# One written order from the attention's end on: routing ahead of dense products, and two batches' gathered expert chains in pieces between them

## The chip, the cores and the metric

The kernel runs on one core of a Trainium2 chip. The metric is the time of one execution on the device, in microseconds; several executions are made and the median is given. A profile is one execution taken by the hardware profiler: its span is the time from its first to its last instruction.

## The reference

Input `x` is 4 batches of 1024 tokens with 128 features, all in float32. Four residual blocks follow each other, each on the layer norm of `x`:

```python
x = x + attention_a(layernorm(x))   # causal softmax, 16 heads of 64, projected back to 128
x = x + ffn(layernorm(x))           # mixture of 32 experts, two per token
x = x + attention_b(layernorm(x))   # linear attention: 16 heads of 8, running sums over all 1024 tokens
x = x + ffn(layernorm(x))           # the same experts and router again
```

The expert block routes every token by a softmax over 32 logits and keeps the two largest weights. Written plainly it sums over all experts, with a weight that is zero for 30 of the 32:

```python
rw = softmax(x @ router_w.T)                 # tokens x 32
vals, idx = top_k(rw, 2)
w = zeros_like(rw).at[rows, idx].set(vals)
out = sum(x * w[:, e:e+1] @ W[e] for e in range(32))
```

Linear attention of a batch needs, at token t, the sums over all tokens up to t of that batch. The second expert block of a token needs only that token.

## The kernel before, in words

`x` lives in SBUF as one tile `x_sb`: 32 chunks of 128 tokens, eight to a batch. Four chunks are a quad (quads 0 to 7, two per batch). The program has four parts, one after the other.

**Softmax attention** (lines 489 to 837) is written in an order made by hand (`manual_schedule`). While it works on a batch, the expert block of the batch before runs between its pieces: `experts` (L214) is a generator, and each `next` issues a small step of it. A chain of `experts` has these steps: statistics and normalization (L226 to L248), router logits (L256), softmax and the two largest (L264 to L284), counting tokens per expert (L290 to L307), the place of each token in a list sorted by expert (L312 to L356), the scatter of each token's row, scaled by its weight, to its two places in a DRAM buffer `xs_d` (L374 and L384), then a pass in groups of four tiles of 128 rows, 47 tiles in all (L402 to L444: load rows, load expert weights, transpose, multiply, store to `ys_d`), then the gather of two rows per token back to `x_sb` (L449). Scatter and gather are indirect transfers issued by POOL, one for each of 16 (chunk, choice) pairs; they are put in a list `queue` and issued one at a time by whoever pops it. The pass may be held by one chain at a time (`passing`). All state of a chain is in a `Room`, of which there is one. When the attention ends, batch 2's chain has 15 of its 16 gathers left in `queue`; these gathers add to `x_sb` in the transfer itself.

**f**: the last two quads (6 and 7, batch 3) have no attention to hide under, and are done densely by `moe` (L860). For each quad it normalizes and transposes (`normed_T`, L130), computes the router and the two weights per token (L886 to L912), and then for each of its four chunks multiplies by all 32 experts, in eight products of 128x512 (four experts each, L922, each with a bank of PSUM, five banks in turn). Products 1, 4 and 6 are scaled by ACT into a tile `t` (L930) that POOL adds up (L944 to L946) and DVE adds to `x_sb` (`settle`, L871); the other five are accumulated in `x_sb` by DVE, four instructions each (L937). Between products a callback issues pieces: `fill` advances the first two `prepare` (L971, features of the linear attention for a quad: statistics L977, POOL's L983 to L986, ACT's L992, products L1010, exp, sigmoid and log with their table loads L1025 to L1033, POOL's L1039 and L1040, DVE's L1045) and pops `queue`.

**lin**: for each chunk u in order, POOL forms the outer products `kv` (L1085), PE adds them to running sums in PSUM (L1103 and L1111), DVE multiplies by the query, reduces (`num`, L1132) and divides, PE projects, and DVE adds to `x_sb` (L1152). `prepare` of later quads runs beside it. This part too has an order by hand.

**s**: the second expert block. `moe` takes quads 2 to 7 densely, 192 products, and one chain of `experts` takes batch 0. Each product issues one pop of `queue` and, when the queue is short, one step of the chain. Here the gathers go to tiles `y` of a pool `came`, and DVE adds them (L476, L481); batch 0's output is stored by L482, a dense quad's by L874.

In f and s `moe` is not under `manual_schedule`: there the layer that records the program decides the order of instructions on each engine, and it may also put work of s into lin where its inputs are ready. Each engine works through its own instructions strictly in that order. A pool's tile is taken again only when the last use of its earlier tenant is done; `reuse_waits="tile"` says that this wait is kept tile by tile.

Of the kernel before, what the change touches and what calls it, by code (L numbers as in the profile page):

```python
# [15 lines left out]
P = 128  # L16
# [4 lines left out]
def hybrid_kernel(  # L21
# [107 lines left out]

    def normed_T(pool, xnp, c0, n, nm, known=None):  # L130

        mv, rstd = known or statistics(c0, n, nm)
        xn = xnp.tile([P, n, D], F32, tag=f"xn{n}", bufs=8 // n, name=f"xn_{nm}")
        xnT = xnp.tile([P, n * P], F32, tag=f"xnT{n}", name=f"xnT_{nm}")
        for c in range(n):
            nc.vector.tensor_scalar(
                xn[:, c, :], x_sb[:, c0 + c, :], mv[:, c, 0:1], rstd[:, c : c + 1],
                ALU.subtract, ALU.mult,
            )
        for g in range(0, n, 4):  # L140
            pt = pool.tile([P, 512], F32, tag="ps1", name=f"pxn_{nm}_{g}")
            for c in range(4):
                nc.tensor.transpose(pt[:, c * P : (c + 1) * P], xn[:, g + c, :], ident)
            nc.scalar.copy(xnT[:, g * P : (g + 4) * P], pt)
        return xnT
# [711 lines left out]
    TB = 12  # L857
    ACT_GROUPS = (1, 4, 6)

    def moe(nm_, store, first=0, between=None, known=(), lag=0):  # L860
        with ExitStack() as ph:
            xnp = ph.enter_context(tc.tile_pool(name=f"xnp{nm_}", bufs=2, reuse_waits="tile"))
            mp = ph.enter_context(tc.tile_pool(name=f"mp{nm_}", bufs=3, reuse_waits="tile"))
            ps_1 = ph.enter_context(tc.tile_pool(name=f"mps1{nm_}", bufs=3, space=PSUM, reuse_waits="tile"))
            ps_e = ph.enter_context(tc.tile_pool(name=f"mpse{nm_}", bufs=5, space=PSUM, reuse_waits="tile"))
            due = []

            def settle(keep):
                while len(due) > keep:
                    xs, s, done = due.pop(0)  # L870
                    nc.vector.tensor_tensor(xs, xs, s[:, :D], ALU.add)  # L871
                    if store and done is not None:
                        b, r = divmod(done, NB)
                        nc.sync.dma_start(  # L874
                            out=out_v[b, :, r : r + 4, :], in_=x_sb[:, done : done + 4, :]
                        )

            for q in range(first, NT // 4):
                nm = f"{nm_}_{q}"
                c0 = q * 4  # L880
                xnT = normed_T(
                    ps_1, xnp, c0, 4, f"m{nm}", known[q - first] if known else None
                )
                pl = ps_1.tile([P, 512], F32, tag="ps1", name=f"pl_{nm}")
                for c in range(4):
                    nc.tensor.matmul(  # L886
                        pl[:, c * E : (c + 1) * E], xnT[:, c * P : (c + 1) * P], rwT,
                        start=True, stop=True,
                    )
                plv = pl[:, : 4 * E].rearrange("p (c e) -> p c e", c=4)  # L890
                mx = small.tile([P, 4], F32, tag="mx", name=f"mx_{nm}")
                nc.vector.tensor_reduce(mx, plv, AX.X, ALU.max)
                ex = mp.tile([P, 4, E], F32, tag="ex", name=f"ex_{nm}")
                nc.vector.tensor_tensor(
# [11 lines left out]
                for c in range(4):  # L906
                    nc.vector.max(m8[:, c, :], rwx[:, c, 0:E])
# [7 lines left out]
                for c in range(4):  # L915
                    xs = x_sb[:, c0 + c, :]
                    parts = []
                    for g in range(E // 4):
                        if between:
                            between(ps_1)  # L920
# [310 lines left out]
```

## Time and profile before

| what | us |
|---|---|
| median of three runs (lowest, highest) | 2033.25 (2030.45, 2037.73) |
| the profiled execution, its own time | 2037.51 |
| its span | 2035.8 |
| busy in the span: PE, DVE, ACT, POOL | 1890.7, 1482.9, 1234.6, 1139.5 |
| f: from 1482 to the first `cum` product | 1596.5 |
| lin: to the last `x_sb` add of L1152 | 1785.5 |
| s: to the end of the span | 2035.8 |

How to read it: a row of engine sums gives, for a stretch of the span, how long each engine was busy and how many instructions it had; "clock" is the share of TensorE's full clock that was granted. The chain of waits goes back from the last instruction to what released it, and lists what stood on that path. A row of waits says who waited for whom, how long in total, how often, and the longest single wait. In a timeline the bracket at the end of a row is the idle time before it and what ended it. Matrix products in float32 appear as two passes each, transposes as one.

### The profile page before, as it was taken

To read this page: it belongs to the slowest core of one execution; us is meant where nothing else is said; L and a number is where in the kernel's file an instruction comes from. 1 tells how busy PE (TensorE), PEld (TensorE's weight loads), DVE (VectorE), ACT (ScalarE), POOL (GpSimd) and SP (SyncE) were. 2 spreads that over 40 slices of the span, in tenths; PEclk is the share of its full clock that TensorE was granted. 3 is DMA by queue.
4 is the path that set the end of the run, shared out by engine and by line. 5 is a ranking of instruction groups with operands and counts; after the bars stand their busy time and mean duration, and the time that the engine had idled before them with its cause. 6 is when DMAs were issued, how large, how long until landed. Compare 5 with 4: busy or idle time off the path is not lost.

```text
span 2035.8 us, 33636 instructions
## 1 busy us (share of the span) xinstructions
PE 1890.7 (93%) x10066; PEld 1052.5 (52%) x10066; DVE 1482.9 (73%) x4467; ACT 1234.6 (61%) x3889; POOL 1139.5 (56%) x2080
## 2 busy tenths in 40 slices
PE   6999999999999999999999999999958898987898
PEld 3555555555555655555565555556633454543443
DVE  5777776776787677778767676777547678966788
ACT  4766666676677566766766676776526466334344
POOL 3444445444665476556745854675476566655644
PEclk9999999999999999999999999999979999997999
DMA  7000000000003310000131100003230000004300
GB/s 214 1 1 1 1 1 1 1 1 1 1 13 93 92 22 10 1 1 5 54 107 45 18 1 1 1 17 111 80 82 0 0 0 1 0 1 123 101 11 11
DMA packets 111875, 62.54 MB, mean 31 GB/s; under 512 B 5552, under 2 KB 110160, under 8 KB 111568
## 3 DMA queue, kind: packets, MB, share of 16 engines
q1 hardware_dynamic: 101936, 50.43, 8.7%
q0 software_dynamic: 9472, 8.40, 2.1%
q8 instruction: 82, 1.34, 0.3%
q10 hardware_dynamic: 288, 1.57, 0.2%
q14 instruction: 97, 0.79, 0.1%
HBM read 35.60 MB, written 24.77 MB: 30 GB/s over the span
## 4 chain that ended last, share of the span: by engine, by line
PE 64%; DVE 12%; ACT 10%; POOL 9%; issue 3%; DMA 1%; ACTq 0%; SPq 0%; POOLq 0%; DVEq 0%
PE s L598 19%; PE po L704 10%; PE pt L687 10%; PE pe_s L922 6%; DVE nmx L607 5%; ACT p L632 3%; PE pw L719 3%; PE pk L547 3%; POOL x_sb L449 2%; ACT pT L691 2%; PE pe L430 2%; PE pv L561 2%; PE cum L1103 1%; ACT p L637 1%; PE pe_f L922 1%
## 5 line engine op out<-in xcount | busy, mean ns | idle before, releaser
L607 DVE TENSOR_REDUCE nmx<-s 128x2 f32<-128x1024 f32 x512 | 604.5, 1219 | 218.5 <-PE s L598 217.8
L632 ACT ACTIVATE p<-s,nmx 128x512 f32<-128x512 f32 (+3 forms) x640 | 361.2, 575 | 311.8 <-DVE nmx L607 264.5
L598 PE MATMUL s<-kT,qT 64*128 64x512 f32 x2048 | 518.0, 619 | 8.0 <-ACT p L632 4.5
L674 POOL TENSOR_SCALAR p<-p,f,ri 128x512 f32<-128x512 f32 (+3 forms) x768 | 503.8, 673 | 0.9 <-issue 0.6
L687 PEld LDWEIGHTS pt<-ident,p 128*128 128x128 f32 x2304 | 249.9, 141 | 219.1 <-issue 91.1
L687 PE MATMUL pt<-ident,p 128*128 128x128 f32 x2304 | 335.9, 282 | 24.4 <-POOL rs L652 7.1
L691 ACT COPY pT<-pt 128x512 f32<-128x512 f32 (+3 forms) x768 | 324.4, 510 | 11.9 <-PE pt L687 9.6
L656 POOL TENSOR_TENSOR rs<-rs,f 128x2 f32<-128x2 f32 x256 | 52.1, 204 | 438.5 <-ACT f L623 409.1
L704 PE MATMUL po<-pT,va 128*64 128x256 f32 (+1 forms) x2560 | 291.1, 365 | 0.6 <-DVE oT L711 0.6
L598 PEld LDWEIGHTS s<-kT,qT 64*128 64x128 f32 x2048 | 173.3, 185 | 195.4 <-issue 94.2
L637 ACT ACTIVATE p<-s,nmx 128x128 f32<-128x128 f32 x512 | 180.7, 366 | 107.3 <-DVE nmx L607 104.6
L704 PEld LDWEIGHTS po<-pT,va 128*64 128x64 f32 x2560 | 167.0, 136 | 97.2 <-issue 32.6
L922 PE MATMUL pe_s<-we_sb,xnT_ms 128*128 128x512 f32 x384 | 186.4, 630 | 22.9 <-DVE x_sb L937 16.4
L937 DVE SCALAR_TENSOR_TENSOR x_sb<-pe_s,w_s,x_sb 128x128 f32<-128x128 f32 x480 | 141.4, 343 | 19.2 <-PE pe_s L922 14.6
L645 DVE SCALAR_TENSOR_TENSOR p<-p,qtri 128x128 f32<-128x128 f32 x512 | 144.9, 310 | 7.0 <-ACT p L637 3.9
L652 POOL TENSOR_TENSOR rs<-rs 128x2 f32<-128x2 f32 x192 | 43.9, 229 | 186.7 <-DVE ri L665 186.7
L632 ACT ACTIVATION_READ_ACCUMULATOR p<-s,nmx 128x1 f32 x640 | 139.0, 217 | 0.0
L930 ACT ACTIVATE t_s<-pe_s,w_s 128x128 f32<-128x128 f32 x288 | 82.2, 369 | 92.5 <-PE pe_s L922 75.5
L922 PEld LDWEIGHTS pe_s<-we_sb,xnT_ms 128*128 128x128 f32 x384 | 72.2, 199 | 116.3 <-issue 37.4
L944 POOL TENSOR_TENSOR t_s<-t_s,t_s 128x512 f32<-128x512 f32 x48 | 60.9, 1269 | 81.4 <-ACT t_s L930 81.1
L724 DVE TENSOR_TENSOR x_sb<-pw,x_sb 128x128 f32<-128x128 f32 x128 | 36.9, 289 | 79.8 <-PE pw L719 79.7
L719 PE MATMUL pw<-wo_sb,oT 128*128 128x128 f32 x512 | 84.5, 289 | 1.8 <-DVE x_sb L724 1.0
(302 smaller groups left out, 2669.5 us busy)
## 6 DMA issues: line engine op xcount, KB each, us to landing
xs<-xs_d SPq DMA_DIRECT2D x33, 256.0 KB, 3.1
ys_d<-ys SPq DMA_DIRECT2D x33, 256.0 KB, 2.4
we<-_ffn_expert_weights_dram SPq DMA_DIRECT2D x24, 256.0 KB, 3.6
xs_d<-zero SPq DMA_DIRECT2D x2, 3008.0 KB, 17.9
we<-_ffn_expert_weights_dram SPq DMA_DIRECT2D x45, 64.0 KB, 1.8
xs_s<-xs_d SPq DMA_DIRECT2D x11, 256.0 KB, 3.6
ys_d<-ys_s SPq DMA_DIRECT2D x11, 256.0 KB, 3.4
we_sb<-_ffn_expert_weights_dram SPq DMA_DIRECT2D x4, 512.0 KB, 6.0
```

The lines of the kernel that those rows point to most:

```text
L598: nc.tensor.matmul(st[:, h, :], self.qT[rows, self.ib * P : (self.ib + 1) * P], self.kT[rows, j * 512 : (j + 1) * 512], start=True, stop=True,
L607: nc.vector.tensor_reduce(self.nmx[:, i, :], self.s[i], AX.X, ALU.max, negate=True)
L632: nc.scalar.activation(self.p[h][:, at : at + m * P], self.s[i][:, h, : m * P], AF.Exp, bias=bias, accum_out=self.rs[:, i, h : h + 1],)
L637: nc.scalar.activation(self.p[h][:, at + m * P : at + (m + 1) * P], self.s[i][:, h, m * P : (m + 1) * P], AF.Exp, bias=bias,)
L645: nc.vector.scalar_tensor_tensor(d, d, 1.0, qtri, ALU.mult, ALU.mult, accum_out=self.rs[:, 2, h : h + 1])
L674: nc.gpsimd.tensor_scalar(w, w, self.f[:, i, h : h + 1], self.ri[:, h : h + 1], ALU.mult, ALU.mult,)
L687: nc.tensor.transpose(pt[:, c * P : (c + 1) * P], self.p[h][:, (g + c) * P : (g + c + 1) * P], ident,)
L691: nc.scalar.copy(self.pTs[h][:, g : g + m, self.col : self.col + P], pt[:, : m * P].rearrange("p (c i) -> p c i", c=m),)
L704: nc.tensor.matmul(po[h * DH : (h + 1) * DH, c0:256], va[:, jb, h, :], pTs[h][:, jb, c0:], start=(jb == 0), stop=(jb == n - 1),)
L719: nc.tensor.matmul(pw[:, :P], oTs[i][:, c * P : (c + 1) * P], wo_sb[:, pr, :], start=(i == 0), stop=(i == len(prs) - 1),)
L922: nc.tensor.matmul(pe, xnT[:, c * P : (c + 1) * P], we_sb[:, 4 * g : 4 * g + 4, :].rearrange("p e d -> p (e d)"), start=True, stop=True,)
L937: nc.vector.scalar_tensor_tensor(xs, pe[:, e * D : (e + 1) * D], w[:, c, 4 * g + e : 4 * g + e + 1], xs, ALU.mult, ALU.add,)
```

## The change

`moe` and `normed_T` go. Their work is split in two, and everything after the attention stands under `manual_schedule`.

- `routed` is a generator that computes the router of one quad in some 15 to 22 small steps. The router of the next quad is stepped once per dense product, so it lies beside the products of the quad before. Quad 6's is issued in one go at f's start, with one step of the first `prepare` after each of its own; quad 4's is issued two steps per chunk near the end of lin.
- `dense` writes the products: after each, the next router's step and a callback with the number of the product. POOL's sums follow as soon as the second tile is there, and `settle` keeps two chunks in hand.
- In f, each product steps one of two `prepare` in turn, and every fourth pops `queue`.
- In s, quads 4 to 7 are dense (128 products). Batches 0 and 1 are done by two chains, each with a `Room` of its own, stepped together after every second product; seven of eight products pop `queue`. What is left of chains and queue after the last product is issued then.
- The pools of f, lin and s have tile-wise waits; `t` has 9 buffers in f and 12 in s.

Repeated lines and blank steps of the two new functions are left out below.

```diff
-    def normed_T(pool, xnp, c0, n, nm, known=None):
...
-    TB = 12
     ACT_GROUPS = (1, 4, 6)
...
-    def moe(nm_, store, first=0, between=None, known=(), lag=0):
...
+    ctx.enter_context(tc.manual_schedule())
+    rp = ctx.enter_context(tc.tile_pool(name="rp", bufs=2, reuse_waits="tile"))
+    ready = {}
+
+    def routed(q, nm, pool, known=None):
+
+        c0 = q * 4
...
+            yield
+            yield
+            yield
+        else:
+            mv, rstd = known
...
+        pt = pool.tile([P, 512], F32, tag="ps1", name=f"pxn_{nm}")
+        for c in range(4):
+            nc.tensor.transpose(pt[:, c * P : (c + 1) * P], xn[:, c, :], ident)
+        nc.scalar.copy(xnT, pt)
+        yield
+        yield
+        yield
+        yield
...
+        mx = small.tile([P, 4], F32, tag="mx", name=f"mx_{nm}")
+        nc.vector.tensor_reduce(mx, plv, AX.X, ALU.max)
...
+        nc.scalar.activation(ex, ex, AF.Exp)
+        yield
+        yield
...
+        nc.vector.tensor_tensor(w[:, :, 0:E], rwx[:, :, 0:E], w[:, :, 0:E], ALU.subtract)
+        ready[q] = xnT, w
+
+    def dense(nm_, qs, store, pool, mp, ps_e, known, beside):
+
...
+        turn = 0
+        for i, q in enumerate(qs):
+            xnT, w = ready.pop(q)
+            nxt = iter(())
+            if i + 1 < len(qs):
+                nxt = routed(qs[i + 1], f"{nm_}_{qs[i + 1]}", pool, known[i + 1])
+            for c in range(4):
+                xs = x_sb[:, q * 4 + c, :]
+                parts = []
+                for g in range(E // 4):
...
+                    if g in ACT_GROUPS:
+                        t = mp.tile([P, 512], F32, tag="t", name=f"t_{nm_}_{q}_{c}_{g}")
...
+                        parts.append(t)
+                        if len(parts) > 1:
+                            nc.gpsimd.tensor_tensor(parts[0], parts[0], t, ALU.add)
+                    else:
...
+                    if g == 3:
+                        settle(2)
+                    next(nxt, None)
+                    beside(turn)
+                    turn += 1
...
+                due.append((xs, s, q * 4 if c == 3 else None))
+            for _ in nxt:
+                pass
+        settle(0)
...
-    def fill(pool):
-
-        banks[0] = pool
-        turn[0] += 1
-        if turn[0] in (4, 18):
-            preps.append(prepare(len(preps), pool))
-        if turn[0] % 2:
-            for p in preps:
-                next(p, None)
-        elif turn[0] > 8:
+    def on():
+
+        for e in list(sides):
+            if len(queue) <= 4 and next(e, "end") == "end":
+                sides.remove(e)
+
+    with ExitStack() as ph:
+        mp = ph.enter_context(tc.tile_pool(name="mpf", bufs=9, reuse_waits="tile"))
+        ps_f = ph.enter_context(tc.tile_pool(name="ps_f", bufs=3, space=PSUM, reuse_waits="tile"))
+        ps_e = ph.enter_context(tc.tile_pool(name="ps_ef", bufs=5, space=PSUM, reuse_waits="tile"))
+        banks[0] = ps_f
+        preps = [prepare(t, ps_f) for t in range(2)]
+
+        def fill(turn):
+
+            next(preps[turn % 2], None)
+            if turn % 4 == 3:
+                if queue:
+                    queue.pop(0)()
+                on()
+
+        qs = list(range(NT // 4 - 2, NT // 4))
+        for _ in routed(qs[0], f"f_{qs[0]}", ps_f, known[0]):
+            next(preps[0], None)
+        dense("f", qs, False, ps_f, mp, ps_e, known, fill)
+        for p in preps:
+            for _ in p:
+                pass
+        while sides or queue:
             if queue:
                 queue.pop(0)()
-            for e in list(sides):
-                if next(e, "end") == "end":
-                    sides.remove(e)
-
-    turn, preps = [0], []
-    moe("f", False, NT // 4 - 2, fill, known)
-    for p in preps:
-        for _ in p:
-            pass
-    assert not (sides or queue) and len(preps) == 2
+            on()
 
     with lin as ph:
-
-        ph.enter_context(tc.manual_schedule())
-        lp = ph.enter_context(tc.tile_pool(name="lp", bufs=3))
-        ps_c = ph.enter_context(tc.tile_pool(name="ps_c", bufs=1, space=PSUM))
-        ps_n = ph.enter_context(tc.tile_pool(name="ps_n", bufs=1, space=PSUM))
-        ps_1 = ph.enter_context(tc.tile_pool(name="ps_l", bufs=4, space=PSUM))
+        lp = ph.enter_context(tc.tile_pool(name="lp", bufs=3, reuse_waits="tile"))
+        ps_c = ph.enter_context(tc.tile_pool(name="ps_c", bufs=1, space=PSUM, reuse_waits="tile"))
+        ps_n = ph.enter_context(tc.tile_pool(name="ps_n", bufs=1, space=PSUM, reuse_waits="tile"))
+        ps_1 = ph.enter_context(tc.tile_pool(name="ps_l", bufs=4, space=PSUM, reuse_waits="tile"))
...
+        qs = list(range(NB // 4 * 2, NT // 4))
         kv = products(0)
-        ends = []
+        ends, first = [], iter(())
...
             ahead(3 * u + 2)
-
-    def pieces(pool):
-
-        banks[0] = pool
-        if queue:
+            if u == NT - 8:
+                first = routed(qs[0], f"s_{qs[0]}", ps_1)
+            next(first, None)
+            next(first, None)
+
+    for _ in first:
+        pass
+    for b, r in enumerate((room, Room(xp, "b"))):
+        sides.append(experts(b, f"s{b}", banks, queue, r, came))
+
+    def pieces(turn):
+
+        if turn % 8 != 7 and queue:
             queue.pop(0)()
-        for e in list(sides):
-            if len(queue) <= 4 and next(e, "end") == "end":
-                sides.remove(e)
-
-    for b, r in enumerate((room,)):
-        sides.append(experts(b, f"s{b}", banks, queue, r, came))
-    moe("s", True, NB // 4, pieces, lag=3)
-    assert not (sides or queue)
+        if turn % 2 and sides:
+            on()
+
+    with ExitStack() as ph:
+        mp = ph.enter_context(tc.tile_pool(name="mps", bufs=12, reuse_waits="tile"))
+        ps_s = ph.enter_context(tc.tile_pool(name="ps_2", bufs=3, space=PSUM, reuse_waits="tile"))
+        ps_e = ph.enter_context(tc.tile_pool(name="ps_es", bufs=5, space=PSUM, reuse_waits="tile"))
+        banks[0] = ps_s
+        dense("s", qs, True, ps_s, mp, ps_e, [None] * len(qs), pieces)
+        while sides or queue:
+            if queue:
+                queue.pop(0)()
+            on()
```

## The prediction, before the result was known

> **What bounds the kernel now.** I read the page's parts 1 to 4 for the stages, then engine sums by stretch, waits, and timelines of POOL, SP and PE. The change starts where the attention ends, at 1482 us. Three stages follow: dense experts of the last two quads ("f", 1482 to 1596.5, when the first `cum` matmul starts), linear attention ("lin", to 1785.5, the last `x_sb` add of L1152), and the second expert stage ("s", to 2035.8). A "turn" is one dense product, 128x512, in the trace two PE passes.
>
> ```profile
> 1482.00:1500.00 18.00, 9.13 (x22) 4.86 (x22) 8.86 (x57) 0.90 (x2) 13.94 (x11) 0.77 0.88 200
> 1500.00:1520.00 20.00, 8.63 (x14) 3.66 (x15) 5.10 (x17) 6.97 (x21) 17.62 (x32) 0.52 0.22 27
> 1560.00:1580.00 20.00, 13.80 (x28) 5.30 (x27) 14.16 (x44) 10.83 (x28) 12.86 (x12) 0.84 0.00 0
> 1740.00:1786.00 46.00, 39.47 (x137) 23.48 (x136) 44.57 (x106) 12.08 (x27) 25.49 (x15) 0.99 0.00 1
> 1820.00:1840.00 20.00, 12.05 (x32) 5.27 (x32) 12.05 (x53) 6.08 (x19) 15.82 (x26) 0.83 0.07 20
> 1840.00:1860.00 20.00, 15.18 (x27) 6.07 (x28) 9.73 (x33) 9.88 (x34) 16.53 (x18) 0.83 0.13 43
> 1880.00:1900.00 20.00, 18.70 (x100) 12.39 (x99) 12.95 (x39) 7.63 (x20) 3.75 (x4) 1.00 0.77 219
> 1960.00:1980.00 20.00, 19.56 (x51) 8.74 (x50) 17.28 (x66) 10.76 (x37) 11.13 (x12) 1.00 0.05 14
> ```
> Columns: stretch, length, busy us of PE, weight load, DVE, ACT, POOL, granted clock, DMA share, GB/s. f stands still for 35 us while POOL works off 15 accumulating fetches. lin's end is DVE's. In s, 1820 to 1860 is POOL's (route and scatter of batch 0), 1880 to 1900 has the chain's rounds, and the end is PE's.
>
> The chain of waits, its rows for a run of 16 turns and for `num` in lin, then who waited in s:
>
> ```profile
> 1965.48 14.00 PE pe_s L922 x32
> ...
> 1619.37 1.25 DVE num L1132
> ...
> 1644.86 1.25 DVE num L1132
> ...
> 1670.52 1.26 DVE num L1132
> ...
> 1695.52 1.26 DVE num L1132
> ```
>
> ```profile
> POOL t_s L944 <- ACT t_s L930: 81.1, 35, 11.7
> ACT t_s L930 <- PE pe_s L922: 75.5, 59, 8.0
> ```
> Timelines of DVE, POOL (scatter, gather), PE (a round of the chain) and SP:
>
> ```profile
> 2015.24 3.97 DVE L937 SCALAR_TENSOR_TENSOR x_sb<-pe_s,w_s,x_sb 128x128 f32<-128x128 f32 x15 [0.89 <-PE pe_s L922]
> ...
> 1840.22 0.96 POOL L374 DMA_INDIRECT xs_d<-xw_s,row_s  x1 [0.30 <-issue]
> 1841.48 0.96 POOL L374 DMA_INDIRECT xs_d<-xw_s,row_s  x1 [0.30 <-issue]
> ...
> 1905.22 0.94 POOL L449 DMA_INDIRECT y_s<-ys_d,row_s  x1 [0.30 <-issue]
> 1906.47 0.95 POOL L449 DMA_INDIRECT y_s<-ys_d,row_s  x1 [0.30 <-issue]
> ...
> 1870.05 0.60 PE L441 MATMUL pxs_s<-ident,xs_s 128*128 128x128 f32 x4
> ...
> 1871.38 1.16 PE L430 MATMUL pe_s<-we_s,xsT_s 128*128 128x128 f32 x8
> ...
> 1887.80 0.38 SPq L436 DMA_DIRECT2D ys_d<-ys_s  x1
> ...
> 1891.16 0.38 SPq L436 DMA_DIRECT2D ys_d<-ys_s  x1
> ```
> A turn is 14.00/16 = 0.87 us of PE; an accumulate 3.97/15 = 0.265 us of DVE, so a chunk (20 of them and a 0.29 settle) 5.6 us; its sums on POOL are 2x1.27+0.74+0.46 = 3.74. A scatter or gather comes every 1.26 us. A round of the chain (four tiles) costs PE some 0.45+0.97 = 1.4 us, from start to start. The waits say that POOL is mostly early; the stalls in s are bursts.
>
> **f stage.** Work is the same; its order changes. The 15 fetches no longer stand first on POOL but one per 4 turns, so `nb_l` no longer waits behind them (ACT waited 19.3 us for it, DVE 8.6). Against that the first router is written with 15 steps of `prepare`, and ACT's transposed copy stands behind four `xn_l`, the router's exp behind four product evictions (1.33 each) and two 1.1 us activations, then a sigmoid and a log with table loads (1.28 each). Adding these from DVE's 1484.4, dense work starts near 1505. Then POOL carries 30 (8 chunk sums) + 27 (15 fetches at about 1.75, from 1.59 and a gap) + 13 (L1019, L1039, L1040, statistics) = 70 us; PE 61, DVE 61. Before ran 58 turns in the 77 us from 1520: 1.33 a turn, 85 us for 64. Between 70 and 85 I take 78: 1505+78+3 (last sum, 2.1 of `kv`) = 1586. **Gain 10** (3 to 18).
>
> **lin.** Order unchanged. Removed are what the scheduler had hoisted here: 20 statistics, 16 aggregates, four `ve_ms` of 1.28, seven `xn_ms`, chain 0's statistics: 19 us of DVE. But `num` came every 25.3 us per four chunks both before and after these appear, so most filled idle time. Added is quad 4's router (6 us DVE), in the last eleven steps, exactly where DVE is full. I take **0** (gain 5 to loss 4). Tile-wise pool releases show no row: bounded by the 0.9 us for which `kv` waited for the last settle, and below by nothing; taken as 0.
>
> **s stage.** The places are read from the order of the built program. Removed: 64 turns (56 us of PE), 45 of DVE, 30 of POOL. Added: batch 1's chain. The written order fixes what lies where: both chains step together every second turn, batch 0's last round falls at turn 123, and **batch 1's twelve rounds and all 32 gathers come after the last turn**.
> - Turns 0 to 47: the second room's clears cost POOL 3x0.41+0.34+0.4, under 2.5 us, in its slack. DVE has 122 accumulates 32.3, settles 1.2, one and a half routers 8.9, both chains' statistics, maxima and replaces 13.7: 56, with some waits 60. PE needs 42, so DVE sets it.
> - Turns 48 to 67: counts, offsets, places. POOL for two chains: 6.1+5.5+5.0+2.9+4.6 = 24, chunk sums 9.4; of the DVE, PE and ACT links between, some 5 stays visible: 38.5. DVE stands in its queue before `big` and `pos` with the accumulates behind it, then PE stands with five full banks.
> - Turns 68 to 98: until batch 0's last scatter POOL issues 24 (8 are batch 1's): 30.2, three chunks' sums 11.2; landing 2.2, SP's issue 0.4, `xs` landing 3.6: 47.7. PE would need 27. ACT can't run ahead: `xw` has eight buffers, so each new four wait for scatters four to eight back, and the evictions queue behind.
> - Turns 99 to 127: 29x0.87 + 12x1.43 = 42.4, say 43; DVE 33, transfers 786 KB in 3.1 us.
> - The tail. A round moves 786 KB; the busiest slice of the stage moved 280 GB/s at nine tenths or more, so 2.7 us; before's rounds came at 2.33 with four of twelve weight tiles loaded beforehand. The last four rounds load weights singly: SP's own issue took about 3.4 (the two last rows). So 3+7x2.7+4x3.4 = 35.5; copy and last store landed 3.5; 16 gathers 20.2; landing 2.6; add 0.8; 512 KB store 3.6: **66**. Batch 0's 16 gathers fit beside the rounds.
>
> Against the tail the Trainium skill has a rule (TensorE: Matmul & The Clock Gate, Part 1: The HAM clock gate): PE runs at half rate until it has been busy for about 3.4 us. In the tail it is busy 1.4 of 2.7. By the rows a round stays at 2.7; by the rule its PE work doubles to 2.8 and also lengthens the chain transpose-copy-product: an estimate of 2 to 4 us more. Rows near it show 0.83 to 0.84 where PE is 60 to 75% busy, not half. I keep 66 and put the 4 in the range.
>
> Sum: 60+38.5+47.7+43+66 = 255, against 250.3: **loss 5**. Before's rows calibrate it: there PE's sum was some 200 and the stage took 250.
>
> **Total**: -10+0+5 = -5: span 2031, and with 1.7 around the span (2037.5 against 2035.8) about 2032.5. The profiled execution was 4.3 over the median of the three runs; the ratio 0.9975 on 2033.25 gives **2028**.
>
> **Rivals.** (A) Slower: POOL, shared by two chains in lockstep, serializes the middle of s. If no link hides, turns 48 to 67 take 47; if batch 1's scatters all have to pass, 32x1.26 and five chunks' sums give 59+6 = 65 instead of 47.7; PE waiting drops the clock and the rounds take 50. Together +33: 2061. It decides from the point at which the 128 turns take over 199 us (mine 189 plus f's 10). For it: the 16.5 busy POOL us of 1840 to 1860 with one chain. Against: now two turns, not one, lie between steps.
> (B) Clearly faster: spreading pays more. f reaches its POOL bound (8 more), lin gains the whole 5, the tail runs at before's 2.33 (4): -17, 2011. For it: DVE's, POOL's and PE's sums for the 128 turns are all near 150, against my 189. Against: these sums peak at different times.
> (C) Nothing moves because the stall of f only shifts: fetches at one per 4 turns keep POOL full to the end, so f ends at 1593; with s at +5 the time is 2035.
>
> **How the numbers follow.** The measurement can tell 0.3%, 6 us, from no change. The middle case with (C), 2017 to 2039: 0.36, of which 0.16 lies below 2027. (B) and beyond: 0.26. (A) and beyond: 0.38; queue waits that I miss all add, so it is wide. Faster 0.42, same 0.20, slower 0.38. The range leaves 0.07 below 2003 and 0.13 above 2056; the middle case's own is 2017 to 2039.
>
> **What would show it.** f: the first `cum` at 1586, POOL over 85% busy from 1505, fetches spaced. lin: `num` spacing kept, DVE full at its end. s: POOL full and PE half idle for some 45 us of scatters, batch 1's first `xs` load when dense work is nearly done, then 66 us with DVE and ACT nearly idle; 16 gathers back to back before the last store. Wrong if the tail is under 55, if the 128 turns take under 170 or over 205, or if lin moves by over 6.

## The result and the profile after

The changed kernel takes 2080.05 us (median of four runs, 2078.10 to 2081.01) against 2033.24 before in the same runs: ratio 1.0227, 95% interval 1.0207 to 1.0247. It is slower by 47 us; 2028 with a range of 2003 to 2056 had been predicted. The profiled execution took 2080.5 us, its span is 2078.8.

The bounds of lin, by the line of its first running sum and then by that of its add to `x_sb` (columns: count, shortest, median and longest duration in ns, first and last start in us):

```profile
L1144 PE MATMUL cum<-kv,mtri x192: 486/486/1009, 1587.1 to 1769.6; 128*128 128x384 f32 x192
```

```profile
L1193 DVE TENSOR_TENSOR x_sb<-lpw,x_sb x32: 273/281/284, 1608.8 to 1776.4; 128x128 f32<-128x128 f32 x32
```

f ends at 1587.1 (predicted 1586). lin lasts to 1776.7, 189.6 us against 189.0 (predicted: no change). All of the loss is in s: 302.1 us against 250.3, predicted 255. The same stretches as before, and some of s:

```profile
1482.00:1500.00 18.00, 13.24 (x34) 6.28 (x34) 4.02 (x20) 9.43 (x26) 3.88 (x6) 0.72 0.00 0
1500.00:1520.00 20.00, 14.13 (x38) 6.68 (x38) 17.04 (x59) 13.23 (x34) 10.07 (x11) 0.83 0.03 5
1560.00:1580.00 20.00, 16.07 (x32) 5.24 (x32) 18.10 (x48) 6.84 (x24) 18.51 (x18) 1.00 0.17 21
...
1820.00:1840.00 20.00, 16.25 (x45) 7.41 (x45) 17.00 (x65) 7.54 (x25) 10.51 (x13) 0.95 0.00 0
1840.00:1860.00 20.00, 13.56 (x33) 6.94 (x32) 16.36 (x80) 4.53 (x15) 9.72 (x12) 0.76 0.05 14
1880.00:1896.00 16.00, 8.51 (x10) 3.27 (x11) 15.26 (x45) 4.68 (x16) 11.98 (x15) 0.50 0.00 0
...
2000.00:2020.00 20.00, 13.35 (x60) 11.75 (x60) 3.53 (x6) 2.34 (x4) 11.39 (x12) 0.54 0.91 258
2020.00:2040.00 20.00, 15.36 (x63) 12.76 (x61) 4.87 (x8) 3.52 (x6) 3.78 (x4) 0.52 0.58 163
2056.00:2076.00 20.00, 0.00 (x0) 0.00 (x0) 2.77 (x4) 0.00 (x0) 11.86 (x13) 0.50 0.21 62
```

f works where it had stood still (DVE 17.04 in the second row, 5.10 before). In s PE is idle for a third of 1840 to 1860 and for almost half of 1880 to 1896, and its granted clock falls there (0.76, 0.50). DVE is busy most of the time, in the last of these rows 15.26 of 16 us; whether its work is the limit is tested below. After 2000 DVE and ACT are nearly idle: that is batch 1's pass alone, then its gathers.

What PE waited for from lin's end to batch 0's first scatter (total, times, longest):

```profile
PE pe_s L949 <- DVE x_sb L966: 7.6, 1, 7.6
PE pxn_s L879 <- DVE xn_s L868: 7.0, 5, 2.0
PE pe_s L949 <- ACT t_s L957: 5.1, 5, 3.5
PE pc_s L281 <- POOL cnta L275: 5.0, 1, 5.0
```

The second and fourth rows are not products: PE stands in its order before a router's transpose and before a chain's counts, and the products written behind these stand too. POOL's wait for ACT's tiles is as long as before (there 81.1, 35, 11.7), so POOL is not what is short:

```profile
POOL t_s L963 <- ACT t_s L957: 89.8, 24, 19.8
```

By the boundaries that the prediction had set (all from lin's end): 98.5 us to the first scatter were predicted, 119.4 measured (1896.1); the scatters 47.7, measured 50.3 (`pxs` at 1946.4); the products' last part 43, measured 51.9 (last accumulate ends at 1998.3); the tail 66, measured 80.5. The excesses are 20.9, 2.6, 8.9 and 14.5: together 47.

The first of these has two steps in the prediction, turns 0 to 47 and 48 to 67. Turns 0 to 47 end with DVE's accumulate number 120, which starts at 1849.0 and lasts 0.35:

```profile
L966 DVE SCALAR_TENSOR_TENSOR x_sb<-pe_s,w_s,x_sb x120: 300/351/352, 1778.5 to 1849.0; 128x128 f32<-128x128 f32 x120
```

That is 72.7 us after lin, 60 predicted; from there to the first scatter it takes 46.7, 38.5 predicted. So both steps run over, by 12.7 and 8.2 us.

### The profile page after: what moved, and what is told of

Read it like the earlier page. It is cut to its first block, busy times and chain, and to the rows that moved or that the text cites. A ratio compares the mean times of both kernels' runs of the same rounds, so it can differ in the third digit from the quotient of the medians.

```text
span 2078.8 us, 33608 instructions
## 1 busy us (share of the span) xinstructions
PE 1880.0 (90%) x10083; PEld 1059.5 (51%) x10083; DVE 1487.5 (72%) x4307; ACT 1221.4 (59%) x3833; POOL 1154.2 (56%) x2129
## 4 chain that ended last, share of the span: by engine, by line
PE 59%; DVE 17%; ACT 9%; POOL 8%; issue 4%; DMA 2%; SPq 1%; ACTq 0%; POOLq 0%; DVEq 0%
PE s L581 19%; PE po L687 10%; PE pt L670 10%; DVE nmx L590 6%; DVE x_sb L966 4%; ACT p L615 4%; PE pw L702 3%; PE pk L530 3%; ACT pT L674 2%; PE pe_s L949 2%; PE pe L413 2%; PE cum L1144 2%; ACT p L620 1%; PE pv L544 1%; PE cum L1152 1%
## 5 line engine op out<-in xcount | busy, mean ns | idle before, releaser
L674 ACT COPY pT<-pt 128x512 f32<-128x512 f32 (+3 forms) x768 | 324.1, 509 | 12.7 <-PE pt L670 10.3
L949 PE MATMUL pe_s<-we_sb,xnT_s 128*128 128x512 f32 x256 | 140.4, 694 | 24.0 <-ACT t_s L957 16.3
L966 DVE SCALAR_TENSOR_TENSOR x_sb<-pe_s,w_s,x_sb 128x128 f32<-128x128 f32 x320 | 111.2, 349 | 43.0 <-PE pe_s L949 32.6
L949 PEld LDWEIGHTS pe_s<-we_sb,xnT_s 128*128 128x128 f32 x256 | 53.6, 224 | 91.0 <-issue 39.4
L963 POOL TENSOR_TENSOR t_s<-t_s,t_s 128x512 f32<-128x512 f32 x32 | 40.9, 1279 | 89.9 <-ACT t_s L957 89.8
L702 PEld LDWEIGHTS pw<-wo_sb,oT 128*128 128x128 f32 x512 | 68.7, 190 | 28.8 <-ACT pT L674 12.5
```

The source lines that it names most:

```text
L674: nc.scalar.copy(self.pTs[h][:, g : g + m, self.col : self.col + P], pt[:, : m * P].rearrange("p (c i) -> p c i", c=m),)
L702: nc.tensor.matmul(pw[:, :P], oTs[i][:, c * P : (c + 1) * P], wo_sb[:, pr, :], start=(i == 0), stop=(i == len(prs) - 1),)
L949: nc.tensor.matmul(pe, xnT[:, c * P : (c + 1) * P], we_sb[:, 4 * g : 4 * g + 4, :].rearrange("p e d -> p (e d)"), start=True, stop=True,)
L966: nc.vector.scalar_tensor_tensor(xs, pe[:, e * D : (e + 1) * D], w[:, c, 4 * g + e : 4 * g + e + 1], xs, ALU.mult, ALU.add,)
```

## The experiments

The kernel before ran beside each group, with medians of 2032.9 to 2035.1.

**Is it the second chain or the written order?** Four kernels. One chain:

```diff
-        qs = list(range(NB // 4 * 2, NT // 4))
+        qs = list(range(NB // 4, NT // 4))
...
-    for b, r in enumerate((room, Room(xp, "b"))):
+    for b, r in enumerate((room,)):
```


> The changed kernel with one chain only: batch 0 by the chain, quads 2 to 7 dense (192 products instead of 128), everything still in the written order. Theory S (the second chain is the loss: two chains in step fill POOL and the links between engines, and the twelve rounds of the second stand alone at the end): f's gain of 9.4 us stays, s needs no tail of rounds and is paced by PE (192 x 0.87 plus 12 rounds of 1.4 = 184 busy us), so s takes 225 to 250 us and the kernel 2000 to 2030 us. Theory W (the written order itself is the loss: engines that work strictly in order stand behind links that the scheduler used to move): s stalls in the same way, 1.64 us for each of the first 70 products as in the changed kernel, and the kernel needs 2050 us or more.

Measured 2058.3 (ratio 1.0119, 1.0103 to 1.0136). Theory W. With one chain the written order is still 25 us slower than before, although f gains 9; there is no tail of rounds in it.

Two chains under the scheduler (edit of the kernel before; the first two lines stand at the end of `moe`):

```diff
+            while store and (sides or queue):
+                between(ps_1)
...
-    for b, r in enumerate((room,)):
+    for b, r in enumerate((room, Room(xp, "b"))):
...
-    moe("s", True, NB // 4, pieces, lag=3)
+    moe("s", True, NB // 4 * 2, pieces, lag=3)
```


> The kernel before, its scheduler kept in f and s, but with the second chain: batches 0 and 1 by two chains with a room each, quads 4 to 7 dense, one step of each chain and one pop of the list after every product; what is left follows the last product. Theory S: s loses as in the changed kernel, and f does not gain: 2070 to 2095 us. Theory W: the scheduler keeps the engines fed and the two chains cost no more than the 64 products they replace: 2025 to 2045 us.

Measured 2038.25 (1.0032, 1.0022 to 1.0042): W again. Under the scheduler the second chain costs 5 us, in the written order 22 (2080.05 less 2058.3).

Without batch 1's chain (only the second pair of lines of the first diff):

> The changed kernel without batch 1's chain: batch 1's second expert block is left out and its rows of the output are not written; 128 products and batch 0's chain remain. The difference to the changed kernel is the whole price of the second chain. Theory S: at least 100 us go (82 of them the tail), the 128 products end 175 to 190 us after lin instead of 220: 1955 to 1980 us. Theory W: the products still stall behind the one chain and the routers and end some 205 us or more after lin, only the tail goes: 1985 to 2000 us.

Measured 1992.83: the time is W's. The products end 193 us after lin instead of 221.6, between the two forecasts, and the first scatter comes after 96.9 us instead of 119.4. So one chain already holds the products back, and the second adds to it.

Steps after every product (`if turn % 2 and sides:` becomes `if sides:`):

> The changed kernel with the two chains stepped after every product instead of every second. Theory S with the tail as its main part: the rounds of batch 1 come earlier and part of them lies beside products, but links that had two products between steps now have one, so stalls grow: tail shorter by 20 to 40 us, products longer by 10 to 25, sum 2050 to 2075 us. If the links (in-order waits) are the main part: slower than the changed kernel, 2085 us or more.

Measured 2073.6 (1.0192, 1.0172 to 1.0212), inside the first forecast, but by luck: the tail is shorter by 75 us, not 20 to 40, and the products are longer by 67, not 10 to 25. The tail of rounds is gone, and the products take it over. PE's waits for a chain's counts and for its normalized rows, 5.0 and 1.8 us to the first scatter in the changed kernel, become

```profile
PE pc_s L281 <- POOL cnta L275: 12.2, 1, 12.2
PE pxn_s L227 <- ACT xn_s L231: 11.5, 3, 9.5
```

**What does the scheduler do better?** DVE's timelines show one thing, in the one-chain kernel late in s (start, length, count):

```profile
2010.28 6.15 DVE L966 SCALAR_TENSOR_TENSOR x_sb<-pe_s,w_s,x_sb 128x128 f32<-128x128 f32 x16
2016.34 0.28 DVE L931 TENSOR_TENSOR x_sb<-x_sb,t_s 128x128 f32<-128x128 f32 x1
2016.54 7.75 DVE L966 SCALAR_TENSOR_TENSOR x_sb<-pe_s,w_s,x_sb 128x128 f32<-128x128 f32 x20
```

20 accumulates take 7.75 us, 0.387 each, against 15 in 3.97, 0.265, in the row of before that the prediction used. A single one lasts about 0.345 in both kernels: it is the spacing that differs. Read from the programs: each accumulate waits for the last write to the same chunk; the scheduler had mostly alternated accumulates of two chunks, the written order does four on one. Two kernels test it, both with the products of two chunks in turn, `c` and `c + 1`; in the second the loops over `e` and `k` are exchanged, and nothing else:

```diff
+                        for e in range(4):
+                            for k in range(2):
+                                xs = x_sb[:, q * 4 + c + k, :]
                                 nc.vector.scalar_tensor_tensor(
...
                     if g == 3:
-                        settle(2)
+                        settle(0)
```


> The changed kernel with its products written for two chunks at a time: product g of chunk c, then of chunk c+1, and DVE's accumulates of the two alternate, so that two that follow each other do not write the same chunk of x_sb. Theory I (interleaving): an accumulate straight behind one on the same chunk takes 0.385 us, as 16 in 6.15 show in the one-chain kernel, and 0.265 behind one on another chunk, as 15 in 3.97 show in the kernel before, whose scheduler had mixed two chunks. Then 320 accumulates of s save up to 38 us of DVE, most of it on the path until the tail: 2042 to 2058 us. Theory L (links: PE stands in its order behind the routers' transposes and the chains' steps, whatever the accumulates cost): 2070 to 2085 us.

> The control of the run with pairs: the same products in the same order, two chunks at a time, but DVE does four accumulates of the first chunk and then four of the second. Only the order of DVE's accumulates differs. Theory I: accumulates stay at 0.36 to 0.385 us and the time stays where the changed kernel is, 2070 to 2088 us. If the order of the products is what helps, it is as fast as the run with pairs.

Measured 2079.62 (1.0231, 1.0213 to 1.0248) and 2084.53 (1.0253, 1.0236 to 1.0270). Alternating is worth 5 us over its control and nothing against the changed kernel: theory L there. DVE's accumulates fall from 111.2 to 87.5 us, and the time does not follow. The front shows why. From lin's end to the changed kernel's first scatter, first the changed kernel, then the run with pairs:

```profile
1776.00:1896.00 120.00, 92.14 (x227) 41.95 (x226) 98.63 (x382) 45.61 (x152) 64.23 (x92) 0.81 0.01 3
```

```profile
1776.00:1896.00 120.00, 90.41 (x233) 41.29 (x232) 90.33 (x392) 45.95 (x156) 65.36 (x95) 0.87 0.01 4
```

DVE, the busiest engine of the front, has 8 us less to do, and the first scatter comes 117.8 us after lin instead of 119.4. Turns 0 to 47 take 69.5 us and the rest of the front 48.3. With one chain the time does follow:

> One chain (batch 0), 192 products, written order, with alternating accumulates of two chunks. Theory I: the one-chain kernel was bound by DVE (8 us per chunk at 0.385 against PE's 7); now PE is the bound, and 25 to 45 us go: 2013 to 2033 us. Theory L: 2045 us or more.

Measured 2043.38 (1.0048, 1.0031 to 1.0065): 15 us less than one chain with serial accumulates, but not the 25 to 45 of theory I.

f and lin written, s as before (moe, its scheduler and one chain put back; the order by hand ends after lin):

> The written order in f and lin only, and s as in the kernel before: one chain, 192 products, and the scheduler free to mix. If the loss lies in s alone and f's gain of 9.4 us is real, the kernel is faster than before by 6 to 11 us: 2022 to 2027 us. If the gain of f is given back, because the scheduler had used the time under f and lin for the statistics of s: 2030 to 2036 us.

Measured 2024.67 (0.9959, 0.9945 to 0.9973). f's gain is real and stays; the loss is s alone.

**The products by themselves.** The loop that adds the two chains is left out, first with serial, then with alternating accumulates:

> The changed kernel without both chains: the second expert block of batches 0 and 1 is left out and their rows of the output are not written; f, lin and the 128 products of s with their routers remain. In the changed kernel these products ended 221 us after lin. By the rates of the traces a chunk costs DVE 20 x 0.385 + 0.3 + a quarter of a router's 6 = 9.5 us, PE 7: if serial accumulates set the products' pace they take 140 to 155 us; if DVE is not what sets it, 112 to 125.

> The same without both chains (batches 0 and 1 left out), with alternating accumulates of two chunks. A chunk costs DVE 20 x 0.265 + 0.3 + 1.5 = 7.1 us, PE 7: the products take 115 to 130 us, 20 to 30 less than with serial accumulates. If the difference is under 6 us, as in the full kernel, the accumulates were never on the path.

Measured 1938.05 and 1908.48 (two executions each), both inside the forecast for accumulates that set the pace. From lin's end to the last accumulate 151.8 and 122.6 us. DVE, serial and then alternating:

```profile
L966 DVE SCALAR_TENSOR_TENSOR x_sb<-pe_s,w_s,x_sb 128x128 f32<-128x128 f32 x320 | 110.8, 349 | 12.9 <-PE pe_s L949 1.0
```

```profile
L971 DVE SCALAR_TENSOR_TENSOR x_sb<-pe_s,w_s,x_sb 128x128 f32<-128x128 f32 x320 | 86.0, 340 | 10.5 <-PE pe_s L950 10.3
```

Columns after the bar: busy, mean ns of one, idle before it. Serial accumulates do set the products' pace when nothing else is there: 30 us. (The products of two chunks in turn with serial accumulates were not run without the chains.) With both chains the products take 221 either way (221.6 serial, 221.3 alternating). So the chains add 70 us to the slow products and 99 to the fast ones: what the chains bring decides, and DVE's sum of accumulates hides under it.

**The links.** Both chains start in lin, nothing else changes:

```diff
+        banks[0] = ps_1
...
+            for b in range(2):
+                if u == NB * b + NB + 3:
+                    r = room if b == 0 else Room(xp, "b")
+                    sides.append(experts(b, f"s{b}", banks, queue, r, came))
+            for _ in range(2):
+                if queue:
+                    queue.pop(0)()
+                if not passing[0]:
+                    on()
...
-    for b, r in enumerate((room, Room(xp, "b"))):
-        sides.append(experts(b, f"s{b}", banks, queue, r, came))
```


> The changed kernel with both chains started in lin: batch 0's from chunk 11 on and batch 1's from chunk 19 on, two steps and two pops per chunk, no round before s. The work is the same, only the long links between engines (statistics to first scatter) lie beside lin, where a step has 3 us for itself. Theory L (in s the engines stand in their order behind those links, then the second chain's rounds come after the last product): lin grows by 8 to 20 us, s loses its slow first 118 us and its tail of 82: 1975 to 2015 us. Theory P (what is short in s is an engine's sum, POOL's 158 us or DVE's 179, wherever the chains start): 2050 us or more.

> The run with early chains, and with DVE's accumulates of two chunks alternating as in the run with pairs. With the links out of the way DVE's sum in s should decide (about 165 us with serial accumulates, 140 alternating, PE 145): 10 to 25 us faster than early chains alone. If alternating still gives under 6 us, the accumulates are not on the path in either kernel.

Measured 2026.63 (0.9966, 0.9952 to 0.9980) and 2012.88 (0.9906, 0.9889 to 0.9922). The first is 53 us under the changed kernel: theory L, theory P falls. The fronts take their own work from s into lin, but lin and s together, with the same work, last 438 us instead of 492. It lies above the forecast: lin grew by 30 us instead of 8 to 20, and s still took 219. Alternating now gives 14 us. Rows of the second, in s:

```profile
1820.00:1840.00 20.00, 19.71 (x109) 13.58 (x109) 18.56 (x51) 11.39 (x37) 17.15 (x24) 1.00 0.82 233
...
1880.00:1900.00 20.00, 18.06 (x101) 12.53 (x100) 13.83 (x41) 7.85 (x22) 13.40 (x15) 1.00 0.83 243
```

Rounds, products, scatters and gathers lie together, PE at full clock; the rounds end 70 us before the last accumulate, and no tail is left but 8 us. This kernel is faster than both, by 20 us against before.

Spreading the chains' steps over lin (one step and one pop at two places of a chunk, from chunks 8 and 16 on):

> Early chains and alternating accumulates, with the chains' steps spread: batch 0's chain from chunk 8 on and batch 1's from chunk 16 on, one step and one pop at two places of each chunk instead of two at its end. In the run before, lin took 217 us instead of 189, with one stall of 7.6 us where DVE waited for a running sum that stood in PE's queue, and batch 1's counts fell into s (PE waited 8.1 us for them). If the links want distance: lin 205 to 215, s 195 to 207, 1993 to 2010 us. If spreading makes no difference to the in-order waits: 2010 us or more.

Measured 2016.23 (0.9906, 0.9890 to 0.9923): the second forecast, in the times no gain on the run before it. lin took 226 us there (217 in the run before it, 190 in the changed kernel) and s 204 (207). What lengthens lin stays open: between 1650 and 1800 DVE waited 21.8 us for running sums that stood in PE's queue in the run with early pairs, against 5.7 in the changed kernel.

One early chain, alternating, and the last comparison, s alone exchanged (f and lin written, two chains under the scheduler):

> One chain (batch 0) started in lin from chunk 11 on, quads 2 to 7 dense (192 products), alternating accumulates, written order. The products alone ran at 0.94 us each (128 in 120.5), so 192 need 181, and 12 rounds of 1.43 lie between them: 198; lin should grow by half of what two chains added, 13. 1775 + 13 + 198 + 5 = 1990 to 2002 us, faster than the two early chains (2013), if links are what the written order pays for and the second chain buys nothing. If the second chain is worth its 64 products: 2013 us or more.

> f and lin in the written order, s under the scheduler with two chains: the changed kernel in all but the order of s. If f's gain adds to the scheduler's two-chain time: 2038 less 9, 2026 to 2033 us; the difference to the changed kernel, some 50 us, is then the price of the written order in s alone. If the written lin takes from the scheduler what it had placed there: 2036 us or more.

Measured 2034.04 (0.9993, 0.9986 to 0.9999) and 2034.14 (0.9997, 0.9988 to 1.0005). The first falls on the side of its second forecast: lin grew by 26 for one chain as for two, and s took 233 us. Two early chains beat one by some 20: the second chain pays once its links are out of the way. The second run, 1 us above its first forecast, differs from the changed kernel in the order of s only: that order costs 46 us. Against the scheduler's two chains with the old f, 1.0032, it shows 7 of f's 9 us.

What "order" holds there is more than the sequence inside s. The chains step after every product in that run; against the written order with such steps (1.0192) 40 of the 46 us remain. And the scheduler had put the statistics of both chains under lin, which was not lengthened by it (184.8 us; DVE's row, 1592 to 1776):

```profile
L209 DVE BATCH_NORM_STATS2 st_s<-x_sb 128x6 f32<-128x128 f32 x16 | 4.5, 281 | 0.0
```

So it began the fronts early too, as the runs with early chains do by hand; its first scatter came 64.8 us after lin. No engine's sum is near the length of s in either kernel: PE 187 and DVE 148 of 256 us there, 204 and 178 of 302 in the changed kernel.

**The tail.** Extra products to keep PE's clock, and transfers of the last tiles in one:

```diff
+            for d in range(2 if passing[0] else 0):
+                pe = ps_e.tile([P, 512], F32, tag="e", name="warm")
+                nc.tensor.matmul(pe, ident, ...)
```
```diff
-                for k in range(g, g + n) if g >= E else ():
-                    e = nc.sync.value_load(...)
-                    nc.sync.dma_start(out=wts[g][:, k - g, :], in_=expert_w[bass.DynSlice(e, 1)]...)
+                else:
+                    nc.sync.dma_start(out=wts[g][:, :n, :], in_=expert_w[g - E : g - E + n]...)
```


> The changed kernel, with two extra 128x512 products, read by nobody, after each step of the tail in which a chain holds the pass (the rounds of batch 1). They add 1.74 us of PE work at full clock to each step and keep PE busy where it waits for the copy of the transposed rows. Theory C (the clock: PE at 0.50 to 0.58 makes a round 3.66 us instead of 2.7): rounds come at 3.0 to 3.3 us, the granted clock of the tail rises over 0.8, and 4 to 8 us go: 2072 to 2076 us. Theory T (the tail's rounds wait for transfers, DMA share 0.9): nothing goes, or the extra products add: 2080 us or more.

> The changed kernel, with the weights of the last fifteen tiles of each chain (the tiles for what overflows) loaded in one transfer of three or four fixed experts instead of one transfer each with the expert read from a register: part of the computation is changed, rows in these tiles are multiplied by experts 0 to 14. If SP's issuing sets the last four rounds of each pass (6.2 us apart against 3.66): 4 rounds of batch 1 come at 3.7, 9 to 11 us less in the tail, and up to 6 at the end of batch 0's pass: 2064 to 2072 us. If they are set by PE and the copies: under 3 us.

Measured 2079.69 (1.0224, 1.0207 to 1.0242) and 2068.32 (1.0168, 1.0151 to 1.0185). A round of the tail in the changed kernel, and with the extra products (PE's timeline):

```profile
2010.09 2.08 PE L413 MATMUL pe_s<-we_s,xsT_s 128*128 128x128 f32 x8 [0.73 <-ACT xsT_s L426]
2011.96 1.06 PE L424 MATMUL pxs_s<-ident,xs_s 128*128 128x128 f32 x4
2013.75 2.08 PE L413 MATMUL pe_s<-we_s,xsT_s 128*128 128x128 f32 x8 [0.73 <-ACT xsT_s L426]
```

```profile
2016.30 1.05 PE L413 MATMUL pe_s<-we_s,xsT_s 128*128 128x128 f32 x8
2017.19 0.60 PE L424 MATMUL pxs_s<-ident,xs_s 128*128 128x128 f32 x4
2017.63 1.88 PE L1256 MATMUL warm<-we_sb,ident 128*128 128x512 f32 x4
2019.35 1.05 PE L413 MATMUL pe_s<-we_s,xsT_s 128*128 128x128 f32 x8
```

Rounds come at 3.05 us instead of 3.66, so transfers were not the limit; the granted clock is 1.00 instead of 0.50. The tail shrinks by 2.4 us only (80.5 to 78.2), since the extra work fills the round. Theory C holds for the round and the clock; its 4 to 8 us were not reached, and the time itself shows nothing.

What a round takes at full clock without extra work is in the trace of the other kernel, in rounds ahead of its first changed load, where the code is the same. The four rounds in the changed kernel, then in that one (columns as before), and two of its rounds on PE:

```profile
2008.00:2024.00 16.00, 13.08 (x55) 11.08 (x53) 3.58 (x6) 2.34 (x4) 5.67 (x6) 0.50 0.91 261
```

```profile
2008.00:2020.00 12.00, 7.92 (x56) 6.61 (x55) 3.57 (x6) 2.67 (x5) 5.66 (x6) 0.94 1.03 294
```

```profile
2012.64 1.16 PE L409 MATMUL pe_s<-we_s,xsT_s 128*128 128x128 f32 x8 [0.73 <-ACT xsT_s L422]
2013.63 0.60 PE L420 MATMUL pxs_s<-ident,xs_s 128*128 128x128 f32 x4
2014.97 1.15 PE L409 MATMUL pe_s<-we_s,xsT_s 128*128 128x128 f32 x8 [0.74 <-ACT xsT_s L422]
```

At full clock these rounds come every 2.33 us, at half clock every 3.66. From store to store the four together are 4.1 us shorter, and the clock is the only difference ahead of the changed loads. Why it was granted in one trace and not in the other is open; more work for PE does not explain it, as PE is busy 66% of the time at full clock and 82% at half.

The singles (weights loaded expert by expert) cost more. SP's queue in the last rounds of the changed kernel, and a round of singles in the kernel before:

```profile
2025.94 3.77 SPq L405 DMA_DIRECT2D we_s<-_ffn_expert_weights_dram  x4
2029.82 0.38 SPq L419 DMA_DIRECT2D ys_d<-ys_s  x1
2030.29 0.46 SPq L393 DMA_DIRECT2D xs_s<-xs_d  x1
2031.82 4.13 SPq L405 DMA_DIRECT2D we_s<-_ffn_expert_weights_dram  x4
2036.06 0.38 SPq L419 DMA_DIRECT2D ys_d<-ys_s  x1
```

```profile
1889.12 1.95 SPq L422 DMA_DIRECT2D we_s<-_ffn_expert_weights_dram  x4
```

The reads of the expert's number into a register, in the changed kernel and in the kernel before:

```profile
L402 SPq TENSOR_LOAD <-which_s x15: 275/279/610, 2024.9 to 2044.7; - x15
```

```profile
L419 SPq TENSOR_LOAD <-which_s x15: 262/281/554, 1837.8 to 1846.6; - x15
```

An issue alone takes 0.33 to 0.36 us, in the kernel before 0.36 in the median. In the changed kernel each has its register read straight ahead of it, so they start some 1.15 us apart, 1.1 us pass between the end of `xs` and the first, and it is 6 us from store to store. In the kernel before, the scheduler had made all 15 reads 30 us and more ahead, and four issues span 1.95 to 2.42 us. In one transfer the tail takes 70.1 us, 10.4 less. Since 4.1 of these are the clock's, in rounds ahead of the first single, the singles account for 6.3 at most.

## Why the prediction was wrong

**f and lin: right.** 1587.1 and 189.6 us against 1586 and no change; f alone, with s as before, gave 8.7 us. POOL was busy 69 us in f from 1505 on, as reckoned (70). DVE was busy 72 instead of 61, by the size of the accumulates below; the 78 us taken for f covered it, so that the agreement is within 1 us is partly luck.

**s: the step that failed** is the allowance for waits in the front of the chains, in its words "56, with some waits 60" for turns 0 to 47 and "of the DVE, PE and ACT links between, some 5 stays visible" for turns 48 to 67. It summed each engine's work by stretch, took the fullest engine, and added 4 and 5 us. The two took 72.7 and 46.7 us for 60 and 38.5. In the run with pairs, where an accumulate costs the 0.265 us of the prediction, they still take 69.5 and 48.3: so it is the waits that were too small, and not mainly the work. The reading that fits the runs: in a fixed order a link is waited for by all that is written behind it, on each engine it touches, and these waits add one after the other. Taking the second chain out moved the first scatter from 119.4 to 96.9; starting both chains elsewhere took 53 us off the kernel; handing only s back to the scheduler took 46. All three change when links stand in the queues, the last two with the same work.

**A mis-sized term beside it: 0.265 us for an accumulate.** The row was right for the order it came from, two chunks alternating; the written order gives 0.387. The Trainium skill (VectorE: DVE Perf Modes, sections "The DRAIN you can't avoid" and "Rules for kernel authors") has eight chained copies take the same time with and without waits between them, and advises to count instructions, not waits, with the remark that one which is not held starts earlier. By that rule 20 accumulates cost the same in either order; here the same 20 take 5.3 us (20 x 0.265) or 7.75. For this instruction the remark matters and the rule does not hold; the measurement decides. The term costs 30 us with the products alone, 15 with one chain or with early ones, and 0 to 5 in the changed kernel, where the links covered it.

**The scatters: right** (50.3 for 47.7). Rival A was wrong in these, where it put most of its loss on POOL (65), and right in the two stretches around them: 47 for turns 48 to 67 if no link hides (measured 46.7) and 50 for the rounds beside products (51.9). So its remark on links held, and POOL as the cause did not: it was busy 64 of the 120 us of the front. It also named the point, 199 us for the 128 turns, which were 221.6.

**The tail: right in kind, 14.5 short.** Two terms are mis-sized. "four rounds with singles at 3.4": the first three came about 6 us apart (from store to store), since 3.4 was read from an order in which the register reads had been made early. And "7x2.7": the four rounds ahead of them came at 3.66. The kernel without singles gained 10.4 of the 14.5, of which 4.1 are the clock's and at most 6.3 the singles' (the same singles are part of the 8.9 in batch 0's last rounds, where products ended 4 us earlier without them). The estimate of 2 to 4 us for the clock, by the Trainium skill's rule (TensorE: Matmul & The Clock Gate, Part 1: The HAM clock gate), was put in the range and not in the sum; the trace sides with half rate (clock 0.50 to 0.54, a round's four products 2.08 us instead of 1.05), and four rounds at 3.66 instead of 2.7 are 3.8 us. When PE leaves half rate the rule does not settle here: it stayed there through runs of 2.9 us with gaps of 0.73, and in the other trace it left after a run just as long (2006.7 to 2009.6).

**Settled and open.** Shown is that the order of s costs 46 us at equal work (40 with equal steps), where the better order also begins the chains under lin, and that moving the chains' fronts there by hand wins as much. That it is the waits in PE's and DVE's queues, link by link, is read from the rows of waits and not removed one by one. What sets the clock's state in the tail is open. Why lin grows by 26 to 36 us with early chains, with one as with two, is open.

## What to carry to other kernels

A duration per instruction belongs to an order: before using it for another order, look at what its neighbours were and what had been done ahead of it, and read the spacing of a run, not the mean of one. Both sizes that failed here, 0.265 for an accumulate and 3.4 for a round of singles, were read from the scheduler's order. If a change replaces a scheduler by a written order, price every cross-engine link as a wait for everything written behind it, and give long chains a stage in which each step has time for itself. A pass left over at the end costs its full latency; register reads that its loads need can be made earlier.

## What was unexpected in the hardware

- Accumulates on one 128x128 chunk follow each other every 0.387 us, alternating on two chunks every 0.265, with 0.34 to 0.35 for a single one in both.
- The settling add of the same size took 0.66 us in the mean in the serial products alone and 0.37 in the changed kernel, with single ones up to 1.36 in the first; what held it was not tried.
- A weight tile whose expert comes from a register costs SP some 1.15 us when the read stands straight ahead of its issue; the issue alone is 0.33 to 0.36 and a read 0.28 in the median. A group of fixed ones in one transfer was issued in 0.59 to 1.11.
- The same rounds of four transposes and four products ran at half clock, 3.66 us each, in one trace and at full clock, 2.33, in another, with no work added.
